# Where TensorE's filler work and the whole-sum rows stand in a four-layer graph kernel

## The chip, the core and the metric

The kernel runs on one core of a Trainium2 chip. The core has five engines with queues of their own: TensorE (PE in the profile, with its weight loads under PEld), VectorE (DVE), ScalarE (ACT), GpSimd (POOL) and SyncE (SP, which here only issues transfers). The metric is the device time of one execution in microseconds (us). Lower is better. The changed kernel is timed beside the kernel before.

## The reference, cut to what matters

There are 2708 nodes with 128 features and one dense weighted adjacency matrix `adj` of 2708 x 2708, about 29 MB in float32. Four layers run one after the other, each with a residual and a layer norm:

```python
x = layernorm(x + L0(x, adj))   # D^-1/2 (adj + I) D^-1/2 x, then W0 and b0
x = layernorm(x + L1(x, adj))   # attention: den = exp(leaky_relu(s_row_i + s_col_j))
x = layernorm(x + L2(x, adj))   # hyperbolic layer: adj @ log(h)
x = layernorm(x + L3(x, adj))   # (adj>0) @ x, (adj<0) @ x and adj @ x, each with its weights
```

In layer 0, `D` is the row sum of `adj + I`, so the degrees of a block of nodes have to be known before its products can be scaled. In layer 1, the weight of edge (i, j) is `den[i, j] / (adj @ den)[i, j]`, and the result is `adj @ (att @ XW)`.

## The kernel before, in words

`adj` is held transposed in DRAM and cut into blocks of 128 rows and columns of 512 (`BW`), so that there are `NB = 6` column blocks (the last has 148 columns) and `NT = 22` tiles of 128 nodes. Work is issued to five in-order queues by a tile framework that places semaphores and may move an instruction ahead of others where no dependency and no `issue_after` forbids it. The helper `queued(PE)` chains what is issued inside it behind what was last issued in this way on the same engine.

**First stage (to about 120 us).** A loop over column blocks `c` loads six tiles `A{d}_{c}`. VectorE adds them up into `part` (tile `ut`, lines 1247 and 1249, then 945 and 946). `degrees(c)` multiplies the sum by a column of ones on TensorE (tile `deg`, line 951), ScalarE takes the root (962), VectorE inverts it and scales this block's rows of `z` (963 to 966, tile `q_b`). `multiply` (931) then forms the products of `z` with the tiles into the six accumulators `acc[0]` to `acc[5]`; `row_products(c - 1)` forms those of the tiles that were kept from earlier columns. "The second degrees" are those of `c == 1`.

**Keys and lists (to about 230 us).** The attention of layer 1 depends on two keys per node. VectorE sorts the nodes into bins and 24 groups (tiles `jk`, `c`, `val`, `pos`, `slot`). Two lists are then made, `i = 0` and `i = 1`: for each of the 22 tiles `t`, VectorE writes a 0/1 matrix `ohs` (line 1483, a ring of 10 buffers), and TensorE multiplies it with `val` into `list` (line 1485). From list 0 come the row numbers `row_i`, with which POOL gathers rows of `adj` (tile `rows_g`, line 1583); from list 1 come the node numbers for `xw_g` (line 1593) and the factors `gj_l`, which four transposes spread over a tile (`gb_first`, line 748). ScalarE makes the first weight matrices of it (`w_first`, line 751), and the grouped attention begins with `num` (line 1632).

**The whole sum.** Apart from that, TensorE forms one row vector, the sum of `e1` times all rows of `adj` (tile `t1`, line 869, written `t` in the profile). The tiles `A` and `B` of `adj` are its operand. One call `sum_rows(1)` takes one tile of 128 rows: up to nine products, each with a single output row, at output partitions 0, 32, 64 and 96. These rows are spread over the stage by hand; where all rows of a block are done, its place is given to the next transfer. The last twelve stand behind the two lists:

```python
                sum_rows((4,8)[i])
                if i == 0:
                    sums_out(sums_of[:3])
```

The four behind list 0 use the tiles `B3` of column blocks 0, 1, 2 and 5. Of the eight behind list 1, four use `B2` and a part of `ut`, four use `B3`, both of column blocks 3 and 4. `sums_out` copies the finished sums to `carry0`, which the first gathered rows need.

**Grouped attention, layers 2 and 3 (to the end).** 48 groups of gathered rows, then products with `adj` tiles (`cb`) in an order that a planner with estimated costs writes (`play`, `resume`, `spend`). The very last work is the layer norm of the last column block, `norm_even` with `b == NB - 1`: square on ScalarE (2101), eight products with a 32-column mean matrix (`st_l`, 2106), root (2114), reciprocal (2115), a spread by the identity on TensorE (`pr_l`, 2123), one product on VectorE (2130), and the transfer out.

Of the kernel before, what the change touches and what calls it, by code (L numbers as in the profile page):

```python
# [10 lines left out]
F32 = mybir.dt.float32  # L11
# [10 lines left out]
P = 128  # L22
NT = (N + P - 1) // P
NP = NT * P
BW = 512
NB = (N + BW - 1) // BW
# [49 lines left out]
def rows(t):  # L76
    return min(P, N - t * P)


def width(b):  # L80
    return min(BW, N - b * BW)


def tiles(b):
    return range(b * (BW // P), min(NT, (b + 1) * (BW // P)))
# [3 lines left out]
def kernel(  # L89
# [20 lines left out]
    nc = tc.nc  # L110
# [3 lines left out]
    psum = ctx.enter_context(tc.tile_pool(name="psum", bufs=1, space=bass.MemoryType.PSUM))  # L114
# [4 lines left out]
    ones = const.tile([P, P], F32, tag="ones", name="ones")  # L119
# [11 lines left out]
    ones_b = const.tile([P, P], BF16, tag="ones_b", name="ones_b")  # L131
# [81 lines left out]
    def acc_tile(b, name):  # L213
        return psum.tile([P, BW], F32, tag=f"acc{b}", name=name)
# [40 lines left out]
    def a_row(pool, k):  # L255

        t = pool.tile([P, N], F32, tag="as", name=f"as{k}")
        nc.sync.dma_start(out=t[: rows(k), :], in_=adjT[k * P : k * P + rows(k), :])
        return t

    def column_sums(dst, sq, b, w_col):

        for t in tiles(b):
            o = t * P - b * BW
            nc.tensor.matmul(dst[:, t : t + 1], lhsT=sq[:, o : o + P], rhs=w_col, start=True, stop=True)
# [553 lines left out]
    kept = {}  # L819
# [86 lines left out]
    with tc.tile_pool(name="tri", bufs=1) as tp:  # L906
# [4 lines left out]
        acc = [acc_tile(b, f"a0_{b}") for b in range(NB)]  # L911
# [14 lines left out]
        def multiply(d, c, t, ks=None):  # L926

            w = width(c)
            for k in ks or tiles(d):
                i, kw = k - tiles(d)[0], rows(k)  # L930
                nc.tensor.matmul(  # L931
                    acc[c][:, :w],
                    lhsT=z[:kw, k, :],
                    rhs=t[:kw, i, :w],
                    start=c not in begun,
                    stop=(d == NB - 1 and k == NT - 1),
                    skip_group_check=True,
                )
                begun.add(c)

        def degrees(c, part):

            w, ts = width(c), tiles(c)
            n = len(ts)
            nc.vector.tensor_add(part[:, :2, :w], part[:, :2, :w], part[:, 2:, :w])
            nc.vector.tensor_add(part[:, 0, :w], part[:, 0, :w], part[:, 1, :w])
            pd = ps_tile(f"deg{c}")
            full = [t for t in ts if rows(t) == P]
            for i, t in enumerate(ts):
                kw = rows(t)  # L950
                nc.tensor.matmul(
                    pd[:kw, i : i + 1], lhsT=part[:, 0, i * P : i * P + kw], rhs=ones[:, 0:1], start=True, stop=True
                )

            span = slice(ts[0], ts[-1] + 1)
            dc = dcol[:, span]
            root = c_tile(f"droot{c}", n)
            if len(full) < n:
                nc.gpsimd.memset(root, 1.0)
            ends = [(P, 0, len(full))] + [(rows(ts[-1]), n - 1, n)] * (len(full) < n)  # L960
            for kw, ia, ib in ends:
                rooted = nc.scalar.activation(root[:kw, ia:ib], pd[:kw, ia:ib], AF.Sqrt, bias=one_c[:kw, :])
            nc.vector.scalar_tensor_tensor(dc, root, 0.0, root, op0=ALU.is_equal, op1=ALU.add)
            nc.vector.reciprocal(dc, dc)
            nc.vector.scalar_tensor_tensor(dc, root, 0.0, dc, op0=ALU.not_equal, op1=ALU.mult)
            scaled = nc.vector.tensor_mul(z[:, span, :], z[:, span, :], dc.unsqueeze(2).to_broadcast([P, n, F]))  # L966
            for kw, ia, ib in ends:
                nc.vector.tensor_copy(row_sum[:kw, ts[0] + ia : ts[0] + ib], pd[:kw, ia:ib])
            return scaled.ins, [rooted.ins]
# [17 lines left out]

        def row_products(c):
            for e in range(c + 1):
                multiply(c, e, kept[c, e])  # L990

        def centred(blocks):

# [215 lines left out]
        def sum_rows(n):  # L1209
            with queued(PE):  # L1210
                whole_sum(n)
# [20 lines left out]
        for c in range(NB):  # L1232
            w = width(c)
            part = ut[:, : 4 * BW].rearrange("p (t c) -> p t c", c=BW)
            at = {}
            for d in range(NB):
                at[d] = load_tile(d, c)
                nt = len(tiles(d))
                if d < NB - 2:
                    check(d, c, at[d])  # L1240
                    if (d, c) == (1, 0):
                        with tc.issue_after(checks[d, c]):
                            load_later()
                if d == 1:

                    with tc.issue_after(scaled) if scaled is not None else nullcontext():
                        nc.vector.tensor_add(part[:, :, :w], at[0][:, :, :w], at[1][:, :, :w])
                elif d > 1:
                    nc.vector.tensor_add(part[:, :nt, :w], part[:, :nt, :w], at[d][:, :nt, :w])  # L1249
                if d < c:  # L1250
                    multiply(d, c, at[d])
                if d >= min(c, NB - 2):
                    kept[d, c] = at[d]
            scaled, rooted[:] = degrees(c, part)
            for d in range(NB - 2, NB):
                check(d, c, at[d])
            if c < NB - 2:
                unit(c)
            if 0 < c < NB - 1:
                row_products(c - 1)  # L1260
            if c == 2:
                prepare_finish()
# [52 lines left out]
    with ctx_keep:  # L1315
# [11 lines left out]
        with tc.tile_pool(name="sort", bufs=1) as st_p:  # L1327
# [11 lines left out]
            with queued(PE):  # L1339
                nc.tensor.matmul(  # L1340
                    lim_v, lhsT=upper, rhs=filled_b[:, :, 1:], start=True, stop=False, skip_group_check=True
                )
                for q in range(1, BQ):
                    nc.tensor.matmul(
                        lim_v[:, :, q],
                        lhsT=ones_b,
                        rhs=filled_b[:, :, before[q - 1]],
                        start=False,
                        stop=(q == BQ - 1),
# [87 lines left out]
            for i in range(2):  # L1437
                for h, (ta, tb) in enumerate(((0, t_a), (t_a, NT))):
                    low[i, h] = acc_tile(2 + 2 * i + h, f"low{i}_{ta}")
                    nn = (tb - ta) * GM  # L1440
                    with queued(PE):
                        nc.tensor.matmul(
                            low[i, h][:, :nn],
                            lhsT=upper,
                            rhs=oh[i][:, ta:tb, :],
                            start=True,
                            stop=False,
                            skip_group_check=True,
                        )
                        for t in range(tb - 1):  # L1450
# [3 lines left out]
                                lhsT=ones_b,  # L1454
                                rhs=oh[i][:, t, :].unsqueeze(1).to_broadcast([P, tb - first, GM]),
                                start=False,
                                stop=(t == tb - 2),
# [10 lines left out]
            for i in range(2):  # L1468
# [12 lines left out]
                for t in range(NT):  # L1481
                    ohs = srt([P, P], f"ohs{i}_{t}", BF16, 10, "ohs")
                    nc.vector.tensor_scalar(ohs, iota_b, slot[:, i, t : t + 1], None, op0=ALU.is_equal)
                    with queued(PE):
                        nc.tensor.matmul(  # L1485
                            ps[:, : 6 * GM],
                            lhsT=ohs,
                            rhs=val[i][:, t, :, :].rearrange("p n g -> p (n g)"),
                            start=(t == 0),
                            stop=(t == NT - 1),  # L1490
                        )
                sum_rows((4,8)[i])
                if i == 0:
                    sums_out(sums_of[:3])
                lists.append(ps[:, : 6 * GM].rearrange("p (n g) -> p n g", g=GM))
# [309 lines left out]
    def fast_rest(u_sb, pieces, free, scratch_pool, blk):  # L1805
# [290 lines left out]
        def norm_even(q, s, b, out):  # L2096

            w = EVEN[b]
            gw = w // 4
            sq = blk.tile([P, BW], F32, tag="sq", name=f"sq_{q}{b}")  # L2100
            nc.scalar.activation(sq[:, :w], s, AF.Square)
            yield 3.0
            st = scratch(f"st_{q}{b}")
            spend(0.45)
            for i in range(4):
                nc.tensor.matmul(
                    st[32 * i : 32 * i + 32, :gw],
                    lhsT=mean_w[:, :32],
                    rhs=sq[:, i * gw : (i + 1) * gw],
                    start=True,  # L2110
                    stop=True,
                )
            r = blk.tile([P, P], F32, tag="gr", name=f"gr_{q}{b}")[:, :gw]
            nc.scalar.activation(r, st[:, :gw], AF.Sqrt, bias=eps_c)
            nc.vector.reciprocal(r, r)
            two, term = (blk.tile([P, P], BF16, tag=t, name=f"{t}_{q}{b}")[:, :gw] for t in ("two", "term"))
            if b < NB - 1:
                three_terms(two, r, blk.tile([P, P], F32, tag="rest3", name=f"rest3_{q}{b}")[:, :gw], term)
            yield 4.5
            pr = scratch(f"pr_{q}{b}")  # L2120
            spend(0.55)
            for i in range(4):
                nc.tensor.matmul(
                    pr[:, i * gw : (i + 1) * gw],
                    lhsT=(sel[:, i : i + 1] if b < NB - 1 else ident[:, 32 * i : 32 * i + 1]).to_broadcast([P, P]),
                    rhs=two if b < NB - 1 else r,
                    start=True,
                    stop=True,
                )
            nc.vector.tensor_mul(out, s, pr[:, :w])  # L2130
# [560 lines left out]
```

## Time and profile before

| what | us |
|---|---|
| median of 3 runs (lowest to highest) | 836.62 (835.50 to 837.32) |
| the profiled execution, its own time | 837.07 |
| its span, first to last instruction | 835.2 |
| PE busy / DVE busy / ACT busy / POOL busy | 794.5 / 620.3 / 518.2 / 136.8 |
| mean granted TensorE clock | 0.982 |

The profile is of one execution. Its own time is 1.9 us above its span and 0.45 us above the median of the runs. "Busy" counts modelled ends of products, so that a stretch in which short products follow each other with gaps can still look almost full. PEclk is the share of the full clock that TensorE was granted; it is 1.00 or 0.50 in this trace, nothing between.

### The profile page before, as it was taken

How to read it: one execution, taken by the hardware profiler on the slowest of the kernel's cores; microseconds unless marked ns; L12 is line 12 of the kernel's file. 1: busy time of each engine (PE TensorE's matmuls, PEld its weight loads, DVE VectorE, ACT ScalarE, POOL GpSimd, SP SyncE). 2: the span in 40 equal slices, each digit the busy share in tenths (PEclk: the TensorE clock that was granted, in tenths of full speed). 3: DMA queues.
4: the chain of work that ended last, by engine and by line, in shares of the span. 5: the costliest groups of instructions: out<-in, count | busy, mean ns of one | idle time of the engine just before them, and what ended most of it. 6: DMA issues, size and time to landing. Idle time of an engine off the chain costs nothing.

```text
span 835.2 us, 10312 instructions
## 1 busy us (share of the span) xinstructions
PE 794.5 (95%) x3392; PEld 448.5 (54%) x3392; DVE 620.3 (74%) x1456; ACT 518.2 (62%) x927; POOL 136.8 (16%) x173
## 2 busy tenths in 40 slices
PE   4789999998999999999999999999999999999995
PEld 3345454454245555455554455564455766677774
DVE  4787645589479999789996677997588863776774
ACT  4956554214189898789886343686445665666662
POOL 5241000001285663253211000000000000000000
PEclk9799999999899999999999999999999999999997
DMA  9997559089479655436535878795985752856600
GB/s 340 358 383 282 142 55 353 26 305 382 151 250 393 190 169 171 135 100 200 165 102 167 280 264 283 238 348 190 361 287 160 238 180 68 291 188 238 227 27 16
DMA packets 94986, 181.71 MB, mean 218 GB/s; under 512 B 6272, under 2 KB 37396, under 8 KB 94584
## 3 DMA queue, kind: packets, MB, share of 16 engines
q1 hardware_dynamic: 85228, 142.62, 49.9%
q0 software_dynamic: 7680, 34.85, 12.9%
q10 hardware_dynamic: 2016, 3.49, 1.2%
q8 instruction: 29, 0.48, 0.2%
q14 instruction: 33, 0.27, 0.1%
HBM read 176.68 MB, written 4.28 MB: 217 GB/s over the span
## 4 chain that ended last, share of the span: by engine, by line
PE 82%; DVE 9%; DMA 5%; ACT 3%; issue 1%; ACTq 0%; DVEq 0%
PE a L2025 17%; PE num L1632 12%; PE uacc L1725 11%; PE a L931 11%; PE a L2533 7%; PE a L2517 6%; PE a_u L1893 5%; DMA A<-in_adjT_dram 4%; PE a L1893 2%; PE t L869 2%; DVE jk L1395 2%; PE upper L1715 1%; PE pp L2420 1%; ACT ln L1637 1%; PE list L1485 1%
## 5 line engine op out<-in xcount | busy, mean ns | idle before, releaser
L931 PE MATMUL a<-A,q_b 128*128 128x512 f32 (+2 forms) x264 | 110.8, 569 | 4.1 <-DVE q_b L966 2.6
L1637 ACT ACTIVATE ln<-num,inval,occ_l 128x512 f32<-128x512 f32 x144 | 99.1, 725 | 21.8 <-PE num L1632 18.2
L1632 PE MATMUL num<-rows_g,w_all 128*128 128x512 f32 (+1 forms) x252 | 104.5, 542 | 0.0
L1725 PE MATMUL uacc<-att,xw_g 128*128 128x512 f32 (+1 forms) x248 | 99.8, 535 | 2.1 <-issue 1.2
L2517 PE MATMUL a<-mask,node 128*128 128x452 f32 (+1 forms) x252 | 94.7, 458 | 0.0
L1650 DVE COPY rows_g<-num 2x512 f32<-2x512 f32 x132 | 76.9, 611 | 17.8 <-ACT ln L1637 14.7
L2025 PE MATMUL a<-cb,q_b 128*128 128x512 f32 (+1 forms) x222 | 89.5, 540 | 0.0
L2500 ACT ACTIVATE mask<-cb 128x904 fp32r<-128x904 f32 (+2 forms) x66 | 60.8, 922 | 34.7 <-PE a L2517 31.7
L2025 PE MATMUL a<-cb,xw 128*128 128x512 f32 (+1 forms) x196 | 79.6, 532 | 0.0
L1663 DVE SCALAR_TENSOR_TENSOR att<-q_b,e_l,ln 128x1354 f32<-128x1354 f32 x48 | 77.5, 1615 | 0.3 <-ACT ln L1637 0.3
L931 PEld LDWEIGHTS a<-A,q_b 128*128 128x128 f32 (+1 forms) x264 | 47.1, 196 | 54.2 <-issue 48.6
L1632 PEld LDWEIGHTS num<-rows_g,w_all 128*128 128x128 f32 x252 | 45.5, 190 | 48.9 <-issue 37.7
L1697 ACT ACTIVATE att<-att,e_l 128x1354 f32<-128x1354 f32 x48 | 68.2, 1421 | 2.5 <-issue 2.1
L2533 PE MATMUL a<-cb,edge 128*128 128x452 f32 (+1 forms) x150 | 68.9, 543 | 0.0
L1583 POOL DMA_INDIRECT rows_g<-in_adjT_dram,row_i x48 | 49.6, 1034 | 116.9 <-PE num L1632 85.3
L1725 PEld LDWEIGHTS uacc<-att,xw_g 128*128 128x128 f32 x248 | 46.8, 190 | 39.6 <-issue 24.9
L2517 PEld LDWEIGHTS a<-mask,node 128*128 128x128 f32 x252 | 46.1, 189 | 26.6 <-issue 24.3
L1222 ACT ACTIVATE xw<-A 128x2048 f32<-128x2048 f32 (+3 forms) x36 | 57.0, 1582 | 2.8 <-DMA A<-in_adjT_dram 1.9
L2025 PEld LDWEIGHTS a<-cb,q_b 128*128 128x128 f32 x222 | 38.4, 190 | 31.6 <-issue 29.4
L1879 ACT ACTIVATE a_s<-cb 128x512 fp32r<-128x512 f32 x43 | 26.6, 626 | 40.2 <-PE a L1893 28.4
L1249 DVE TENSOR_TENSOR ut<-ut,A 128x2048 f32<-128x2048 f32 (+3 forms) x24 | 43.8, 1824 | 8.9 <-DMA A<-in_adjT_dram 7.9
L1593 POOL DMA_INDIRECT xw_g<-xw_d,xw_i x24 | 43.0, 1792 | 18.8 <-PE gb_first L748 11.8
(550 smaller groups left out, 1318.4 us busy)
## 6 DMA issues: line engine op xcount, KB each, us to landing
cb<-in_adjT_dram SPq DMA_DIRECT2D x10, 2816.0 KB
A<-in_adjT_dram SPq DMA_DIRECT2D x25, 1024.0 KB
cb<-in_adjT_dram SPq DMA_DIRECT2D x10, 2560.0 KB
B<-in_adjT_dram SPq DMA_DIRECT2D x18, 1024.0 KB
cb<-in_adjT_dram SPq DMA_DIRECT2D x5, 2486.0 KB
cb<-in_adjT_dram SPq DMA_DIRECT2D x5, 2260.0 KB
cb<-in_adjT_dram SPq DMA_DIRECT2D x2, 1554.0 KB
cb<-in_adjT_dram SPq DMA_DIRECT2D x1, 2464.0 KB
```

The source lines that it names most:

```text
L931: nc.tensor.matmul(acc[c][:, :w], lhsT=z[:kw, k, :], rhs=t[:kw, i, :w], start=c not in begun, stop=(d == NB - 1 and k == NT - 1), skip_gro ...
L1632: nc.tensor.matmul(num[:, : cb - ca], lhsT=w, rhs=gat[q][:, ca:cb], start=True, stop=True)
L1637: nc.scalar.activation(ln_n[q][:, ca:cb], num[:, : cb - ca], AF.Ln, scale=occ_l[:, g : g + 1], bias=inval[:, g : g + 1],)
L1650: nc.vector.tensor_copy(gat[q + 1][0:2, ca:cb], num[0:2, : cb - ca])
L1663: nc.vector.scalar_tensor_tensor(att[q], q_b[:, h * HALF : (h + 1) * HALF], e2_l[:, g : g + 1], ln_n[q], op0=ALU.max, op1=ALU.subtract,)
L1697: nc.scalar.activation(att[q], att[q], AF.Exp, bias=e1_l[:, g : g + 1])
L1725: nc.tensor.matmul(uacc[h][c][:, : cb - ca], lhsT=xw_g[:, g, :], rhs=att[q][:, ca:cb], start=(g == 0), stop=(g == GM - 1), skip_group_chec ...
L1893: nc.tensor.matmul((acc if j == 2 else upper[0])[:, :w], lhsT=parts[j], rhs=rows3[j], start=(j == 0 and not upper[1]), stop=False, skip_gr ...
L2025: nc.tensor.matmul(acc()[:, :w], lhsT=weights[:, k, :], rhs=a, start=(k == 0), stop=False, skip_group_check=True)
L2500: nc.scalar.activation(mask[:, :n, :w], hold[i][0][:, t : t + n, :w], AF.Sign)
L2517: nc.tensor.matmul(acc()[:, :w], lhsT=node[:, k, j, :], rhs=mask, start=(k == 0 and j == 0 and b != 1), stop=False, skip_group_check=True,)
L2533: nc.tensor.matmul(acc()[:, :w], lhsT=edge[:, k, :], rhs=piece(k), start=(k == 0 and b == 1), stop=False, skip_group_check=True,)
```

## The change

Three edits that touch four places. A helper `keep_busy` issues products of a 128 x 128 matrix of ones in bf16 with itself, 512 columns wide, whose result nobody reads. The first edit puts eight of them ahead of the second degrees, into the accumulator of column block 5, which has not been begun there; the products of the kept tile (`row_products(0)`) are now issued ahead of the degrees in the text too. The second spreads the twelve whole-sum rows: two inside list 0 (after `t` = 7 and 14) and two behind it, four inside list 1 (after `t` = 4, 9, 14 and 19) and four behind it. The third puts ten products of ones into the last norm, five ahead of the mean products and five behind them in the text.

```diff
+    def keep_busy(dst, n):
+
+        for _ in range(n):
+            last = nc.tensor.matmul(
+                dst, lhsT=ones_b, rhs=ones_b.unsqueeze(1).to_broadcast([P, 4, P]), start=True, stop=True
+            )
+        return last.ins
...
-                nc.tensor.matmul(
+                last = nc.tensor.matmul(
                     acc[c][:, :w],
...
+            return last.ins
+
+        busy = {}
...
-                nc.tensor.matmul(
-                    pd[:kw, i : i + 1], lhsT=part[:, 0, i * P : i * P + kw], rhs=ones[:, 0:1], start=True, stop=True
-                )
+                with tc.issue_after(busy[c]) if c in busy else nullcontext():
+                    nc.tensor.matmul(
+                        pd[:kw, i : i + 1], lhsT=part[:, 0, i * P : i * P + kw], rhs=ones[:, 0:1], start=True, stop=True
+                    )
...
         def row_products(c):
             for e in range(c + 1):
-                multiply(c, e, kept[c, e])
+                last = multiply(c, e, kept[c, e])
+            return last
...
+            if c == 1:
+                product = row_products(c - 1)
+                with tc.issue_after(product):
+                    busy[c] = keep_busy(acc[NB - 1], 8)
             scaled, rooted[:] = degrees(c, part)
...
-            if 0 < c < NB - 1:
+            if 1 < c < NB - 1:
                 row_products(c - 1)
...
+                    if t in ((7, 14), (4, 9, 14, 19))[i]:
+                        sum_rows(1)
-                sum_rows((4,8)[i])
+                sum_rows((2, 4)[i])
...
             nc.scalar.activation(sq[:, :w], s, AF.Square)
+            if b == NB - 1:
+                idle = psum.tile([P, BW], F32, tag="acc5", name="idle")
+                keep_busy(idle, 5)
             yield 3.0
...
+            if b == NB - 1:
+                keep_busy(idle, 5)
             r = blk.tile([P, P], F32, tag="gr", name=f"gr_{q}{b}")[:, :gw]
```

In the built program the order of instructions moves on two engines. On TensorE, `row_products(0)` already stood ahead of the second degrees, so the first edit adds only the eight products of ones, between `row_products(0)` and the first product of column block 2. The whole-sum rows move as the text says. In the last norm, seven of the ten products of ones stand ahead of the mean products and three behind. On VectorE, the first two `ohs` of list 1 come among the small operations on list 0 (before: behind them), and the four small operations that make `sc`, `bi` and the start of `w_first` (lines 1525 to 1530) come behind the last `ohs` of list 1 (before: among them). ScalarE, POOL and SP keep their order.

## The prediction

> **What bounds the kernel now.** I read the page first (busy times, clock, chain), then the windows of TensorE around each half-clock slice, then the chain in order of time through the lists and the end.
>
> ```profile
> PE 794.5 (95%) x3392; PEld 448.5 (54%) x3392; DVE 620.3 (74%) x1456; ACT 518.2 (62%) x927; POOL 136.8 (16%) x173
> ...
> PEclk9799999999899999999999999999999999999997
> ...
> PE 82%; DVE 9%; DMA 5%; ACT 3%; issue 1%; ACTq 0%; DVEq 0%
> ```
>
> TensorE is the bound: 82% of the chain. From 240 us to the last norm the waits that end with another engine sum to under 2 us, so whatever makes the start of the attention (`gb_first`, 227.41) earlier should make the end earlier by as much. The clock row dips in three places besides the start; the windows say where:
>
> ```profile
> 40.76:44.17 3.41, 1.86 (x4) 1.00 1.05 389
> 44.17:47.59 3.42, 2.05 (x11) 1.00 1.05 386
> 47.59:51.00 3.41, 3.41 (x5) 0.50 1.06 385
> ...
> 204.60:208.01 3.41, 2.53 (x16) 1.00 1.05 386
> 208.01:211.43 3.42, 3.42 (x23) 0.50 0.52 194
> ...
> 214.84:218.25 3.41, 2.55 (x19) 1.00 0.93 321
> 218.25:221.67 3.42, 3.42 (x27) 0.50 0.95 381
> ...
> 822.41:825.83 3.42, 1.70 (x12) 1.00 0.00 0
> 825.83:829.24 3.41, 2.02 (x8) 0.50 0.03 7
> ```
>
> Columns: stretch, length, PE busy (instructions), granted clock, DMA share, GB/s. Each half-clock stretch lasts 3.41 us or runs to the end, and each follows a 3.41 us window with little real work. Busy overstates it: a 512-column f32 record holds the array 0.43 us and a list product (144 columns, bf16) about 0.06 us, by their spacing when nothing is waited for. Counted so, the windows ahead of the four drops held 0.33, 0.28, 0.28 and 0.34 of real work, while 40.76 to 44.17 held 0.41 and kept its clock. I estimate the limit at 0.35 to 0.41.
>
> ```profile
> 207.18 2.09 PE list L1485 x12
> 209.27 2.26 PE t L869 x9
> ...
> 211.57 2.32 PE t L869 x14
> 213.89 0.58 PE list L1485 x8
> ...
> 217.62 0.40 PE list L1485 x2
> 218.02 0.42 PE t L869 x6
> ...
> 222.76 4.65 PE t L869 x35
> 227.41 0.59 PE gb_first L748 x4
> ```
>
> This is the chain (start, length, what). TensorE first idles through list 0 at VectorE's pace, one `ohs` each 0.163 us, and then pays the rows in series.
>
> **What the Trainium skill says.** "TensorE: Matmul & The Clock Gate", section "What's actually happening": the clock is full or half, decided by a free-running activity window of 3413 ns. The trace agrees (1.00 and 0.50 alone; 3.41 us). It ties the drop to an idle window; here 0.34 of work did not prevent it. The same page, "Back-to-back issue gap", gives 512 columns as 215.7 ns at full and about 427 ns at half clock; no such product is in this trace, and the nearest row (`low` L1452, 20 bf16 products of 480 down to 24 columns in 2.31 us, 0.115 each) fits. "Step-by-step: what each phase is for" has products stay in program order, so an inserted row delays the list products behind it. "The mechanism" (same page, packing) lets products in different column groups run together; the trace agrees, since a row of three 512s and one 148 takes 0.89 us, about two f32 records of 0.43.
>
> **The change part by part.**
>
> *Second degrees.* Added: 8 x 0.216 = 1.73 us of ones. `row_products(0)` ends at 41.49; TensorE then waits to 43.01 for a tile, runs one product (0.86) and waits for VectorE's sum to 45.54. The ones fill 41.5 to 43.2, push that product by 0.2 us, and the degrees still start at 45.54. Cover: the VectorE sum (L945 and L946, 43.31 to 45.39). If it were gone, or the clock half there (8 x 0.427 = 3.4 us), the degrees would slip about 1.1 us. The clock recovered at 37.35, so I take full. The gain: 47.59 to 51.00 at half clock costs 1.71 us of products. But the third degrees wait for VectorE, which ends its sum at 61.10 and does not depend on this clock; they now start at 62.10. So at most **0.9 us** goes through. And the last window, 44.17 to 47.59, is hardly touched by ones that end at 43.2: with windows at the same phase the drop stays (0 gained). Over all phases: a window drops if it holds over 2.15 us of idle (63% of 3.41). With the ones the idle is 44.1 to 46.43, and a window may start from 42.8 to 44.3 for that: 1.5 of 3.41, or 43%. Before, with 41.49 to 43.01 idle as well, it may start from 41.1 to 44.3: 93%. I take **0.4**, bounds -0.3 and 0.9.
>
> *Lists.* Nothing is added; twelve rows move. Their full-clock cost: behind list 0, 209.27 to 213.89 is 4.62 us, less half of the 2.16 us at half clock: 3.54, or 0.89 each. Behind list 1, 218.02 to 223.24 is 5.22, less 1.71: 3.5, or 0.88 each; the last four, 4.17 or 1.04 each. After the change, step by step:
> - List 0 begins at 204.96. Row one runs 206.2 to 207.1 while VectorE writes on in its ring of ten; seven waiting products take 0.0725 each (8 in 0.58 at 213.89). Row two ends near 208.9, the list near 209.4, against 209.27.
> - Two rows: 1.8, to 211.2. VectorE's `ohs` of list 1 come from about 209.9 and 211.2 on; product 4 is done at 212.0.
> - Four rows 3.5, 17 products 1.23, four switches between row and list: a spread between two rows (183.97 to 184.55 for 4 x 0.107) costs 0.15 over its own time, so 0.6. List 1 ends near 217.4.
> - Four rows, 4.2: `gb_first` at **221.5** instead of 227.41. Gain **5.9 us**: 3.2 - 0.1 of half clock not incurred (the windows now hold over half real work), the rest is idle filled.
>
> What is late next? The row tiles: the last two `B3` land at 208.8 and 211.4 and are needed from 217.4; the `B2` and `ut` ones land by 206.1, needed at 211.9. `gj_l` trails the list by 1.6 us: 219.0, hidden. The gathers on POOL wait for `row_i`, which comes behind two `ohs` (0.33) and a list end 0.15 later, so they start near 212.0 instead of 211.60 and land from about 218.3 (four, 1.5 us apart); `num` begins near 222.6. Margin 4 us. The four moved VectorE operations (under 0.7 us together) end by 217 and are needed at 222. POOL's `xw_g` gather waits for `gb_first` and moves with it. SP's queue has nothing behind these rows. Bounds: 3.1 (clock alone) and 6.3 (no switch cost).
>
> *Last norm.* Added: ten ones. The last product ends about 823.55; seven take 1.5 us, to 825.1, against a mean product released at 825.04: 0 to 0.1 lost, the cover being VectorE's sum and ScalarE's square. Three more (0.65) end at 826.1, ahead of 826.86. Their accumulator is free since 822.4 (L1908). Then `pr_l`, 2.04 us at half clock, runs at full: spreads of the same kind take 0.107 each, eight 0.86 + 0.2 = 1.06. Gain **0.95**, bounds -0.2 and 1.0. If the ones ran at half clock (10 x 0.43) the mean products would slip 1.8; 822.41 to 825.83 was at full.
>
> *Sum.* 0.4 + 5.9 + 0.95 = 7.25 from the profiled execution's own 837.07 gives 829.8. That execution had all the drops and stands 0.45 above the median. The changed kernel sheds most of that luck but may meet one of the thin windows near 168 to 177 us (0.43 to 0.49 of work), in either kernel. I add 0.4: **830.2**.
>
> **The rivals.**
> *A, as summed:* 830.2, its own range 828.8 to 831.8.
> *B, the rows fit badly:* ring of ten full, broken column packing, more switch cost, so the lists give the clock and little else: 837.07 - 3.1 - 0.95 = 833.0. For: VectorE waited for PE three times in list 1 (2.1 us). Against: that was behind four rows in series.
> *C, the ones do nothing:* windows drop all the same in both gaps: 837.07 - 5.9 = 831.2. For: the window arithmetic at the second degrees. Against: at the end the idle gap is nearly closed.
> *D, slower:* a switch between column-packed rows and full-array products drains the array. There are twelve switches in the lists; they outweigh A's 6.85 us of lists and norm from 0.57 us above nothing each; at 0.7 it is 837.07 - 6.85 + 8.4 = 838.6. Against: the spread at 183.97, 0.15 for two.
>
> **How the numbers follow.** A 0.62, B 0.18, C 0.15, D 0.04, no visible change 0.01. A difference under 0.2% (1.7 us) is about what a measurement of this kernel can't tell from none. A, B but its worst end, and C are faster by more: 0.93. Same 0.03, slower 0.04. The range 828.6 to 833.4 takes in A, C and B's middle.
>
> **What would show it.** Right: no half clock between 200 and 230 us; `gb_first` at 221 to 222.5 relative to the same list start; `list` products in runs of 5 to 8 with `t` between; `pr_l` near 1.06 us; third degrees near 61.2 where the clock held. Wrong: `gb_first` past 224 with ScalarE or a gather as releaser of `num`; `ohs` waiting for PE for several us; a half-clock window among the ones. If the attention starts 6 us earlier and the end does not, a transfer bounds a later stage and the first paragraph is wrong.

## The result and the profile after

The change is faster, by less than half of what was forecast: 833.28 us median (832.26 to 834.61, 8 runs) against 836.15 (834.39 to 838.46, 8 runs) for the kernel before, ratio 0.9967, 95% interval 0.9952 to 0.9982. That is 2.9 us; the prediction had 6.4. A second comparison (e_after, below) gave 0.9962 (0.9950 to 0.9974), which agrees in size.

The page of the changed kernel, in the three lines that answer to those of before (busy times, clock, shares of the chain):

```profile
PE 794.2 (96%) x3410; PEld 448.7 (54%) x3410; DVE 620.2 (75%) x1456; ACT 517.7 (62%) x927; POOL 136.4 (16%) x173
...
PEclk9899999999999999999999999999999999999999
...
PE 82%; DVE 8%; DMA 5%; ACT 3%; issue 1%; ACTq 0%; DVEq 0%
```

TensorE is still the bound. The 8 in the eleventh slice, at about 208 to 229 us, has become a 9, and so has the 7 in the last. A single stretch of 3.41 us at half clock takes a slice of 20.8 us only to 0.92 and so still shows as a 9; the windows of TensorE, with the same columns as before, show those that are left:

```profile
42.67:46.08 3.41, 1.77 (x11) 1.00 1.05 388
46.08:49.50 3.42, 3.42 (x5) 0.50 1.06 387
165.55:168.96 3.41, 3.41 (x36) 1.00 0.02 5
168.96:172.38 3.42, 3.26 (x31) 0.50 0.41 104
...
206.51:209.92 3.41, 3.41 (x32) 1.00 0.91 334
...
213.34:216.75 3.41, 2.85 (x26) 1.00 0.58 156
...
820.91:824.32 3.41, 2.71 (x22) 1.00 0.01 2
```

The lists and the last norm keep the full clock. The second degrees lose it at 46.08 as they did before, and the window from 165.55, full by its busy time, held only 0.18 of real work (counted by columns, as in the prediction) and was followed by 3.41 us at half clock. The chain of waits through the lists shows what became of the idle time:

```profile
205.28 0.27 DVE ohs L1500
...
206.97 0.96 PE t L877 x5
207.93 0.76 PE list L1502 x7
...
210.20 1.82 PE t L877 x13
212.02 0.24 PE list L1502 x2
...
212.46 0.47 ACT xw L1481
...
214.18 1.02 PE t L877 x2
...
219.41 4.10 PE t L877 x32
223.51 0.60 PE gb_first L756 x4
```

List 0 and the two rows behind it end at 212.02, 0.2 us later than foreseen relative to the list's start. Then the chain leaves TensorE for ScalarE: nine products into list 1, TensorE comes to a row that has to wait for ScalarE. The timeline says for how long (the bracket is idle time and its releaser):

```profile
214.18 1.02 PE L877 MATMUL t<-B,e 128*1 128x512 f32 x2 [0.56 <-ACT xw L1481]
```

These are the three copies of finished row sums (`sums_out`). The one-output row of list 1 writes the accumulator that they read, at other partitions; it waited all the same, so the framework's wait covers the whole tile. Nothing like it is in the trace of before, where the rows stood behind the list.

**Where the time went.** The profiled executions (own times 837.07 and 832.47) differ by 4.6 us: -0.4 up to 168 us (the transfer of an early `A` tile landed sooner), +1.0 from the half clock at 169, -4.5 from the first `ohs` to `gb_first` (22.69 to 18.16), -0.7 in the last norm (5.82 to 5.14, from the last addition to the end of `ob`). From `gb_first` to the last norm both take 596.41. So the 4.6 is real for this pair, and the 2.9 of the medians says that the pair isn't typical: that execution of before had two drops of the clock in the lists and one in the last norm. It did not have every drop that the kernel can meet, as the prediction took it: none came at 165 to 181 us, where 14 of the 18 executions in the table below have one.

### The profile page after: what moved, and what is told of

Its sections match the earlier page's. It is cut to its first block, busy times and chain, and to the rows that moved or that the text cites. A ratio compares the mean times of both kernels' runs of the same rounds, so it can differ in the third digit from the quotient of the medians.

```text
span 830.6 us, 10357 instructions
## 1 busy us (share of the span) xinstructions
PE 794.2 (96%) x3410; PEld 448.7 (54%) x3410; DVE 620.2 (75%) x1456; ACT 517.7 (62%) x927; POOL 136.4 (16%) x173
## 4 chain that ended last, share of the span: by engine, by line
PE 82%; DVE 8%; DMA 5%; ACT 3%; issue 1%; ACTq 0%; DVEq 0%
PE a L2044 17%; PE num L1651 12%; PE a L939 11%; PE uacc L1744 11%; PE a L2557 7%; PE a L2541 6%; PE a_u L1912 5%; DMA A<-in_adjT_dram 4%; PE a L1912 2%; PE t L877 2%; DVE jk L1412 2%; PE upper L1734 1%; PE pp L2444 1%; ACT ln L1656 1%; PE su L301 1%
## 5 line engine op out<-in xcount | busy, mean ns | idle before, releaser
L1602 POOL DMA_INDIRECT rows_g<-in_adjT_dram,row_i x48 | 47.4, 987 | 117.8 <-PE num L1651 85.1
L1899 DVE TENSOR_TENSOR rows_hold<-rows_hold,cb 128x452 fp32r<-128x452 f32 (+1 forms) x51 | 31.6, 626 | 18.6 <-ACT rows_hold L1898 15.1
```

## The experiments

The theory behind the experiments: moving rows fills little, the clock brings most of the gain, and how much depends on where the free-running windows fall in an execution; the ones at the second degrees miss the gap. The rival was the prediction's own sum. Sixteen runs in four groups; each group shared runs of the kernel before on its chip (medians 836.05, 834.55, 836.32, 836.44), so each ratio compares within its own group. Across groups they compare only roughly, for the kernel before did not lose its clock equally often in them. The mean granted clock is known for every run, and one stretch of 3.41 us at half clock takes 0.002 from it (3.41 x 0.5 / 835). Over its runs in the four groups it was 0.9824, 0.9839, 0.9814 and 0.9819. So in the second group the kernel before had about one stretch fewer per run, its median was 1.5 to 1.9 us lower, and the ratios lie nearer to 1; whether by chance or by the chip is not known. The changed kernel did not run in the first two groups.

The stretches of every profiled execution, in us, in the order of time: second to third degrees; third degrees to first `ohs`; first `ohs` to `gb_first`; last addition to the end of `ob`. They are differences of start times in each trace.

| kernel | deg 2 to 3 | deg 3 to ohs | ohs to gb_first | last norm |
|---|---|---|---|---|
| before | 16.40 | 142.7 | 22.69 | 5.82 |
| after | 16.40 | 143.7 | 18.16 | 5.14 |
| e_before | 16.40 | 144.0 | 18.99 | 5.02 |
| e_rows_only | 16.40 | 143.2 | 18.17 | 5.82 |
| e_ones_only | 16.39 | 144.0 | 20.86 | 5.14 |
| e_late_sums | 18.07 | 142.7 | 18.61 | 5.14 |
| e_list_ones | 16.40 | 142.7 | 18.67 | 5.82 |
| e_deg13 | 15.63 | 143.8 | 18.16 | 5.14 |
| e_sums_end | 18.02 | 143.1 | 17.08 | 5.14 |
| e_best | 15.63 | 144.0 | 17.08 | 5.14 |
| e_after | 18.06 | 143.2 | 18.17 | 5.13 |
| e_deg13b | 15.64 | 143.9 | 18.17 | 5.13 |
| e_late_rows | 15.64 | 144.0 | 17.64 | 5.13 |
| e_rows_again | 16.40 | 144.0 | 18.17 | 4.91 |
| e_lr_0 | 15.64 | 145.3 | 17.62 | 5.13 |
| e_lr_8 | 16.40 | 143.9 | 17.62 | 5.14 |
| e_lr_13 | 15.63 | 145.6 | 17.62 | 5.13 |
| e_lr_none | 16.40 | 142.7 | 17.62 | 5.11 |

### Group 1: the parts

**e_before**, the kernel before, unaltered.

> The kernel before, unchanged, as a control that lists span and mean clock of every run. Theory 1 (the profiled execution before was an unlucky one): most runs have a mean clock above 0.982, since each 3.41 us stretch at half clock takes 0.002 from it, and the times fall by roughly 1 us for each stretch that is missing; ratio 1.000 within its interval. Rival (the profiled execution is typical): all runs at 0.981 to 0.983 and the times spread without regard to the clock.

Measured: 834.65 (ratio 0.9989, 0.9978 to 1.0000), 18.99 in the lists without a half-clock stretch. The chain of this execution of the kernel before:

```profile
206.13 0.31 DVE ohs L1483 x2
...
210.68 3.54 PE t L869 x23
214.22 0.91 PE list L1485 x12
...
217.45 1.25 PE t L869 x12
...
225.19 0.60 PE gb_first L748 x4
```

The same code that took 22.69 in the first profile takes 18.99 when the windows fall otherwise; 20.86 with one drop (e_ones_only, whose rows stand as before). One half-clock stretch there costs 1.85. The mean of its 22 runs is 0.9 us below that of the 67 runs of the same kernel beside it, with a mean clock of 0.9835 against 0.9824, about half a stretch fewer per run. So a comparison of one kernel with itself can come out 0.9 us apart, and the place of the windows fits as the cause.

**e_rows_only**, the twelve rows moved, no ones.

```diff
-                with tc.issue_after(product):
-                    busy[c] = keep_busy(acc[NB - 1], 8)
...
-                keep_busy(idle, 5)
...
-                keep_busy(idle, 5)
```

> The rows spread through the lists as in the change, no products of ones anywhere. Theory 1 (the lists bring nearly all of the gain, the ones little): 2.0 to 3.0 us faster than before, and no half clock between 200 and 225 us in the profile; the start of list 0 to gb_first takes about 18.2 us as in the changed kernel. Rival (the list gain is larger and the ones give part of it back): 4 us or more faster than before, that is faster than the change.

Measured: 832.95, ratio 0.9966 (0.9954 to 0.9979), 18.17 in the lists. The rows alone give the whole gain of the change, as e_rows_again below confirms beside the changed kernel. Their mean clock over the 14 runs was 0.9854, against 0.9824 and 0.9835 for the two sets of the kernel before in this group: one to one and a half stretches fewer per run. Against an undisturbed list of before that is 18.99 - 18.17 = 0.8 us of filled idle time, where the prediction counted 2.8.

**e_ones_only**, the ones at both places, the rows as before.

```diff
-                    if t in ((7, 14), (4, 9, 14, 19))[i]:
-                        sum_rows(1)
-                sum_rows((2, 4)[i])
+                sum_rows((4,8)[i])
```

> The products of ones in the degrees and in the last norm, the rows as before. Theory 1: 0.2 to 0.9 us faster than before, all of it at the end: from the last products to the end of the last VectorE product about 5.1 us against 5.8 in the profile before, and the third degrees no earlier than with the half clock that still comes after the second. Rival (the ones cost time): slower than before by 1 us or more.

Measured: 834.59, 0.9989 (0.9976 to 1.0001), no different from the control beside it. The half clock came at 45.6 to 49.0 in spite of the ones, and once in the lists.

**e_late_sums**, the three early copies put behind the rows of list 1.

```diff
-                if i == 0:
+                if i == 1:
                     sums_out(sums_of[:3])
```

> The change, with the first three copies of finished sums (sums_out) issued behind the second list instead of behind the first, so that ScalarE doesn't read the sum's bank while the rows inside list 1 want to write it. Theory 1 (that read holds up the first row inside list 1): the wait of t for ScalarE's copy (0.56 us in the changed kernel at 213.6) is gone, list 0 to gb_first takes 17.0 to 17.7 us instead of 18.23, and the time is 0.5 to 1.1 us below that of the change. Rival (VectorE's pace or the row order holds list 1 anyway): 18.0 to 18.4 us and no difference in time; or the copies become late and num waits for the first rows, which makes it slower.

Measured: 833.68, 0.9973 (0.9961 to 0.9984), 18.61 in the lists: missed. The wait in list 1 was gone, but ScalarE's and TensorE's timelines show a new one:

```profile
222.15 1.78 ACT L1481 COPY xw<-t 1x512 f32<-1x512 f32 x3 [9.47 <-issue]
223.84 0.22 ACT L1538 ACTIVATE gj_l<-list_s 128x24 f32<-128x24 f32 x1
```
```profile
224.10 0.65 PE L756 MATMUL gb_first<-ident,gj_l 128*128 128x128 f32 x4 [1.46 <-ACT gj_l L1538]
```

The copies now started only at 222.15, about where the rows behind list 1 end, and held up `gj_l` behind them in the in-order queue. The wait was passed on from TensorE to ScalarE and back.

### Group 2: clock without fill, more ones, the copies elsewhere

**e_list_ones**, one 128-column product of ones behind each list product, rows as before, no other ones.

```diff
+                warm = acc_tile(2 + 2 * i, f"warm{i}")
...
+                    with queued(PE):
+                        keep_busy(warm, 1)
...
-                sum_rows((2, 4)[i])
+                sum_rows((4,8)[i])
```

> The twelve rows stand behind the two lists as in the kernel before, and no ones run at the second degrees or in the last norm; instead a 128-column product of ones (about 0.05 us) follows each of the 44 list products. That gives TensorE work in the lists' windows without moving anything into its idle time: the clock without the fill. Theory now held: the full clock alone is nearly all that the change brings in the lists, and filling the idle time with rows only 0.8 us; so no half-clock stretch between 200 and 230 us, and from the first ohs to gb_first 18.9 to 19.5 us, where the changed kernel takes 18.17. Rival, the prediction's own sum (2.8 us of filled idle time): about 21.0 us without it. Third: 0.05 us of ones do not count as work, and the half clock comes back: 20.8 with one stretch, 22.7 with two. Whole time 833.6 to 834.7 for the first, 835.5 or more for the others, against about 836 for the kernel before.

Measured: 833.44, 0.9990 (0.9982 to 0.9997), 18.67 in the lists, no half clock. The prediction's sum (21.0) is refuted: without moving a single row into the idle time, but with the clock held, the lists are within 0.5 us of the changed kernel's, and a little below the 18.9 to 19.5 expected. The time shows less, 1.1 us below the kernel before, which in this group lost its clock least often. A sliding window over the undisturbed trace e_before says how often a drop is to be expected there: real work in it falls below 0.36 at 84 of 100 positions of the windows, each time in one window; with the rows moved the lowest is 0.42, with these ones 0.38, at any position. (Real work is counted as in the prediction, by columns.)

**e_deg13**, thirteen ones at the second degrees for eight.

```diff
-                    busy[c] = keep_busy(acc[NB - 1], 8)
+                    busy[c] = keep_busy(acc[NB - 1], 13)
```

> The changed kernel with 13 ones ahead of the second degrees in place of 8. The eight ended at about 42.5 and left 2.7 to 2.9 us of a 3.41 us window with nothing but one-column products; thirteen should end near 43.6 and the product behind them near 44.6, so that no window between 40 and 46 us holds over 1.6 us of idle time. Theory: the number of ones was too small and the clock now holds, so no half-clock stretch between 42 and 52 us; from the second to the third degrees 15.5 to 15.9 us in place of 16.40, and nothing lost at the second degrees, which wait for VectorE to 45.2; 832.4 to 833.0 in all. Rival: the third degrees wait for VectorE and transfers either way, so 16.3 to 16.4 with the clock full; whole time as the changed kernel, 833.3. Third: the ones delay the second degrees by 0.3 to 1 us, and it is slower by that.

Measured: 833.36, 0.9984 (0.9974 to 0.9994); 15.63 between the degrees, no half clock there. The theory on the gap holds, to the tenth; the time does not show it (832.4 to 833.0 was expected). The windows:

```profile
41.12:44.54 3.42, 2.63 (x12) 1.00 1.05 387
44.54:47.95 3.41, 3.41 (x15) 1.00 1.05 387
```

The chain of the same execution shows the prediction's limit at work, VectorE's sum in front of the third degrees:

```profile
58.99 0.84 DVE ut L957
59.96 1.02 PE deg L963 x8
```

**e_sums_end**, all nine copies behind `gj_l` and the first weight matrices.

```diff
-                if i == 0:
-                    sums_out(sums_of[:3])
...
-            sums_out(sums_of[3:])
+            sums_out(sums_of)
```

> The changed kernel with ScalarE's three early copies of row sums moved behind gj_l, to where the other five stand. In the changed kernel the first row inside list 1 waits 0.56 us for these copies; put between the lists' exponentials (the run before with late sums) they held up gj_l and so gb_first by 1.46 us. Theory: with both waits gone the lists close up, from the first ohs to gb_first 17.1 to 17.7 us where the changed kernel takes 18.17, and 596.4 us from there to the last norm as ever: about 0.7 us faster than the changed kernel, 832.4 to 832.9. Rival: the first row waits for nothing but VectorE's one-hots come no sooner, so list 1 ends when it did and the lists stay at 18.0 to 18.2. Third: eight copies in one run hold up ScalarE's first logarithms, and the stretch from gb_first grows by 0.5 us or more, to 597 or above.

Measured: 833.77, 0.9989 (0.9978 to 1.0000). The lists fell to 17.08, more than expected, and `gb_first` to the last norm rose from 596.41 to 599.57. Of these 3.2 us, 1.6 is a half-clock stretch at 226.0 to 229.4 (e_late_sums had the same one and 598.04, and e_best, below, none and 597.99). The rest is in the timelines of TensorE and VectorE:

```profile
226.12 5.88 PE L1649 MATMUL num<-rows_g,w_first 128*128 128x512 f32 x10 [2.14 <-DVE rows_g L1631]
```
```profile
225.65 0.41 DVE L1631 COPY rows_g<-xw 2x512 f32<-2x512 f32 x1 [1.85 <-ACT xw L1481]
```

The first gathered rows (`rows_g`) need exactly these sums, so the first `num` waits 2.1 us for VectorE, and VectorE for ScalarE's copies. It was not the logarithms, as the third case had it, but the copies' readers. The wait was moved a second time.

**e_best**, both edits together.

> Both together: 13 ones ahead of the second degrees and all eight copies of row sums behind gj_l. If both theories hold, about 1.4 us below the changed kernel, 831.6 to 832.3, with no half-clock stretch after the start but the thin windows between 167 and 180 us. If the third degrees wait for VectorE all the same: 832.5. If neither is worth anything: 833.3.

Measured: 834.07, 0.9994 (0.9983 to 1.0005): missed. 15.63 and 17.08 in the trace, so both local gains are there (0.8 and 1.1); given back were 1.6 behind `gb_first` and the half clock at 168.9 and 175.8.

### Group 3: on one chip with the changed kernel

**e_after**, the changed kernel once more.

> The changed kernel itself, unaltered, as the yardstick for the three runs beside it on one chip, and as a second profiled execution of it. Where only the phase of the activity window is drawn anew: 18.1 to 18.2 us from the first ohs to gb_first without a half-clock stretch, 16.40 between the second and third degrees and a half-clock stretch at 42 to 52 us in about two executions of three; the ratio to the kernel before as in the first comparison, 0.9952 to 0.9982.

Measured: 833.39, 0.9962 (0.9950 to 0.9974). Between the degrees 18.06: the half clock lasted two windows.

```profile
42.04:45.45 3.41, 1.48 (x5) 1.00 1.05 387
45.45:48.86 3.41, 3.41 (x10) 0.50 1.05 387
48.86:52.28 3.42, 3.42 (x5) 0.50 1.06 380
```

**e_deg13b**, the thirteen ones again.

> The kernel with 13 ones ahead of the second degrees once more, beside the changed kernel on one chip. If the 0.77 us that its trace showed between the second and third degrees comes through to the end: about 0.8 us below the changed kernel wherever that dropped its clock there, 0.5 on the average of phases, with 15.63 us between these degrees and no half-clock stretch before 160 us. If it is given back later: equal to the changed kernel within 0.3 us.

Measured: 833.47, 0.9969 (0.9952 to 0.9986): equal to the changed kernel, although 15.64 is in the trace. The second of the two expectations, given back later.

**e_late_rows**, thirteen ones, and in list 1 two rows, at products 14 and 18, with six behind the list.

```diff
-                    if t in ((7, 14), (4, 9, 14, 19))[i]:
+                    if t in ((7, 14), (13, 17))[i]:
                         sum_rows(1)
-                sum_rows((2, 4)[i])
+                sum_rows((2, 6)[i])
```

> As the kernel with 13 ones, and in list 1 only two rows lie between the products, behind the 14th and the 18th in place of the 5th, 10th, 15th and 20th, with six behind the list in place of four. ScalarE's three early copies of row sums end about 8.9 us behind the first ohs; the first row of list 1 then comes when they are done, while TensorE goes on with list products at VectorE's pace. Theory: the 0.56 us wait is gone and nothing else is lost, 17.3 to 17.7 us from the first ohs to gb_first in place of 18.16, and 596.4 from there on, since the copies stay where they were: 0.6 us below its neighbour with 13 ones, about 1.1 below the changed kernel. Rival: what TensorE lost waiting it now loses idling at VectorE's pace, 18.0 to 18.2.

Measured: 831.75, 0.9950 (0.9933 to 0.9968), 17.64 in the lists. The chain:

```profile
211.92 1.70 PE list L1502 x10
213.67 0.30 PE list L1502 x2
213.97 1.00 PE t L877 x9
214.96 0.36 PE list L1502 x4
```

TensorE takes list products while ScalarE copies, and the row at 213.97 starts behind them without a wait. 18.17 less 17.64 is 0.53 us, nearly the whole 0.56 of the wait, and it is there in every trace with this order (17.62 to 17.64 in five of five). In the traces, moving fewer rows into the list was better than moving more; the times agree (831.75 and, for e_deg13b, 833.47), but six runs each overlap.

**e_rows_again**, the moved rows without ones, a second time.

> The twelve moved rows without any ones, a second time, beside the changed kernel on one chip: the ones' own worth. By the traces so far the ones of the second degrees change nothing and those of the last norm give 0.68 us where the clock had dropped and cost 0.12 where it had not; so 0 to 0.7 us above the changed kernel. If it is not slower at all, the ones bring nothing, and the rows are the whole change. The prediction's sum had 1.35 us for the ones.

Measured: 832.40, 0.9959 (0.9946 to 0.9972): not slower than the changed kernel on the same chip. The ones as they stand bring nothing that can be measured.

### Group 4: how many ones

All four have the late rows of e_late_rows; they differ in the ones at the second degrees (0, 8, 13) and, in e_lr_none, in that the norm's are gone too. e_lr_13 is e_late_rows again.

> The rows as in the run with late rows (two inside list 1, six behind it), the ten ones of the last norm, and no ones at the second degrees. Five profiled executions without ones there all show one half-clock stretch and 16.40 us between the second and third degrees; of five with eight ones, three show two stretches and 18.0 to 18.1. Theory: eight ones cost about 1 us on the average and thirteen gain 0.8, so here 16.40, one stretch, and a time between those two: about 832.3 to 832.8. Rival: those three executions were chance, and 0, 8 and 13 ones come to the same time within 0.4 us.

> The same with eight ones at the second degrees, as in the changed kernel. Theory: TensorE is idle from about 43.4 to 46 us behind ones that ran too early; where the window that ends between 0.1 us ahead of the degrees and 0.5 us behind them drops the clock, the next one holds less than it takes to recover, and the half clock lasts 6.83 us: 18.0 to 18.1 between the degrees in most executions, 16.40 in the others, and a mean time 0.5 to 1.5 us above the kernel without these ones. Rival: 16.40 or less in each, and the same time.

> The same with thirteen ones, the best version so far, a second time. Theory: 15.63 between the degrees, no half-clock stretch there, 0.8 us below the kernel without these ones up to the third degrees; the clock at 167 to 179 us may take back some 0.5. So 831.6 to 832.3, 1 to 2 us below eight ones. Rival: all of it is taken back, and the time is that of the kernel without ones at the second degrees.

> The late rows without any ones: the norm's ones are left out too. Theory: in the last norm 5.8 us where the clock had dropped, 4.9 to 5.0 where it had not (5.14 with the ones): 0.3 us above the kernel without ones at the second degrees on the average, too little to see in the times. Rival, the prediction's sum: 0.95 above.

Measured, in this order: 832.31 (ratio 0.9957, 0.9942 to 0.9972), 831.90 (0.9953, 0.9935 to 0.9970), 831.16 (0.9948, 0.9928 to 0.9967), 831.58 (0.9950, 0.9931 to 0.9970). The intervals overlap wholly: no number of ones can be told from another by its time. The theory that eight ones cost 1 us isn't borne out: e_lr_8 had one stretch and 16.40, and e_lr_0, without ones, by chance none and 15.64. Over all traces, between the second and third degrees, eight ones gave 16.4 three times and 18.0 to 18.1 three times, no ones 16.4 six times and 15.64 once, thirteen 15.63 or 15.64 five times. Whether eight ones really make the two-window case likelier stays open; thirteen prevented the drop in all five.

And why do thirteen not pay? The table's second column: the six executions in which the clock held at the second degrees took 144.4 on the average from the third degrees to the first `ohs`, the twelve others 143.3. The 0.77 gained is gone by then. The place is the bins, at 165 to 181 us, where small products on the weight-load path fill the busy time and hardly the array. The windows of e_lr_13 there:

```profile
163.60:167.01 3.41, 3.41 (x36) 1.00 0.18 51
167.01:170.43 3.42, 3.42 (x19) 0.50 0.00 0
...
177.25:180.67 3.42, 3.18 (x27) 0.50 1.06 389
```

Four windows in a row at half clock. The four executions without a half-clock stretch there (before, e_late_sums, e_list_ones, e_lr_none) took 142.7 for the table's second column; the fourteen with one took 143.1 to 145.6, and all six that had held the clock at the second degrees are among these. Why the executions that start this stage earlier meet it with the windows in a worse place wasn't tried; six against twelve may still be chance.

## Why the prediction was right and wrong

**Right: the bound and the way through.** TensorE bounds from the lists on, and 3.90 us gained at `gb_first` in the pair of traces were 3.89 us at the last norm, 596.41 in both. Faster came out, as given 0.93, and 833.28 lies in the range, but at its upper end, which was there for rival B. The ones cost what was counted: eight started 0.216 us apart, from 40.77 on. Of the signs, there was no half clock between 200 and 230 us, and rows and list products alternate. `gb_first`, at 222.8 relative to the same list start, missed the 221 to 222.5.

**Wrong: "Lists", 5.9.** Two terms failed. The first is the clock term, 3.1 of it. It was taken from the one execution at hand, which had two drops. Each costs 1.85, so there it was even worth 3.7 (22.69 less 18.99); but with the rows as before the three traces have two, none and one. The mean of 22.69, 18.99 and 20.86 is 20.85, against 18.17: 2.7 us for the whole term. The sliding window gives a size as well: 84% of positions with one drop of 1.85 us are, as an estimate, 1.6 us for the clock, half of the 3.1. The prediction saw that the execution stood 0.45 above the median, and then put only 0.4 for luck and only for another place.

The second is the fill, 2.8 of it, which measured 0.8. Beside the undisturbed e_before, list 0 with its four rows takes 1.35 us less (206.13 to 214.22 is 8.09, 205.28 to 212.02 is 6.74), but list 1 with its eight rows takes 0.5 more (214.22 to 225.12 is 10.90, 212.02 to 223.44 is 11.42). So all the fill came from list 0, and the rows moved into list 1 lost time, because of the wait: where the copies stood behind it (e_sums_end), the lists took 17.08. Step by step from the first `ohs`: list 0 and two rows end after 6.74 us, with 6.55 foreseen (204.65 to 211.2). List 1 ends after 14.13, with 12.75 foreseen: 7.39 for it, not 6.2. There the 1.2 is: 0.56 is the wait for the copies, four rows of 0.99 in place of 0.88 are 0.4, and 0.2 is left without a name. The "what is late next" went through transfers, gathers, `gj_l` and VectorE, and left out the reader of the row's own accumulator, ScalarE's `sums_out`, although the code stands next to the edit. The order of queues alone could not show it, but the trace of before had the copies' lengths, 0.57 each.

More simply, in the undisturbed kernel before, list 1 with its waiting takes 3.23 us (214.22 to 217.45), and 22 products at 0.0725 are 1.6 of it. So at most 1.6 us could be filled there, and the change put four rows of 0.9 in. A full-clock trace shows less idle time than one in which rows at half clock had held up everything.

**Wrong: "Second degrees", 0.4.** The gain was 0 and the limit of 0.9 was right: 0.77 when the clock holds. What failed is the share of phases. TensorE reached the ones at 40.8, not 41.5, since the clock came back at 35.84 and not at 37.35; the ones ran off by 42.5, the product behind them by 43.4, and from there to 46 the array had nothing but one-column products. The prediction let the ones end at 43.2 and had 43% of positions with a drop; the sliding window over the trace after has 66%, and 0% with thirteen ones. It also took a drop to be one window long; three of the six executions with eight ones had two.

**Partly right: "Last norm", 0.95.** The mechanism holds: 1.00 in the window from 820.91 and 5.14 us in all 12 executions with these ones. The spread by the identity, before and after:

```profile
826.89 2.04 PE pr_l L2123 x8
```
```profile
823.22 1.13 PE pr_l L2147 x8
```

That is 0.91 gained, but the seven ones in front made the mean products start 1.51 us behind the last addition instead of 1.29, so 0.22 was lost where at most 0.1 was foreseen, and 0.68 is left. That is for an execution with the drop. Without ones, the one whose clock fell only behind the spread (e_rows_again) took 4.91, so there the ones cost 0.2; in e_before and e_lr_none (5.02 and 5.11) it fell during the spread. The mean of six executions without them is 5.42: the term is 0.3.

**"Sum".** The traces' means give 2.7 + 0.3, and at the second degrees nothing or a little less: about 3.0, or 2.1 if the 0.9 by which the six executions with eight ones are longer there isn't chance. Measured: 2.9, and 3.2 in the second comparison.

**The rivals.** B (rows fit badly, 833.0) came nearest by its number, and its mechanism was half right: the rows gave the clock and little else, for a wait that it did not name. C held for the second degrees and not for the norm. D fell: in the chain rows and list products follow each other without a gap where nothing is waited for, and a row between products takes 0.96 to 0.99 us, against 0.88 to 0.89 alone, not 0.7 more for each switch.

**A faster version**, by the traces, is e_late_rows: 0.53 us less in the lists, in five of five. It took 0.9950 and, again, 0.9948 of the kernel before, with intervals that lie below 0.9970, and without any ones as much (0.9950). That it beats the changed kernel is likely but not shown by time: in the one group with both, the intervals (0.9933 to 0.9968 and 0.9950 to 0.9974) overlap.

## What to carry to other kernels

An effect that depends on where a free-running window falls has to be sized over its positions, by sliding the window over a trace, and never from the drops of one execution; take a second profile of the same kernel before pricing it. When work is put into an idle stretch, count that stretch in an undisturbed execution, and list for every moved instruction who reads and who writes the tile that it touches, not only who feeds it. A small local gain can be real in the trace (0.77 us here) and still not arrive, so follow it past the next two stages.

## What the runs showed of the hardware

The Trainium skill, "TensorE: Matmul & The Clock Gate", "What's actually happening", ties the half clock to an idle window and the full one to a busy window. The traces here grade this. Over the 18 traces, of the windows that began between 38 and 818 us, 36 lost the full clock: 34 held 0.15 to 0.36 of real work and two 0.38 and 0.42, though many were over half busy in the profile. Of those that kept it, two held 0.35 and all others 0.38 or more. So the limit lies near 0.37, by a count of columns that isn't exact to more than some hundredths. To get the clock back more is needed: of the windows at half clock, eleven with 0.42 to 0.77 of work stayed there, and all those that recovered held 0.70 or more, so the two overlap between 0.70 and 0.77. That is why one drop can last two windows or four. Ones that stream through the array count as work: in e_deg13 the window from 41.12 held 0.65 with the thirteen ones, would have held 0.25 without them, and kept its clock. Products of one or two columns hardly count: after the change, 24 of them, 0.11 us apart with weight loads as dense (eight in 0.97 us), filled most of the window from 165.55, which held 0.18 by columns and was followed by half clock.
